# Row maxima of both query halves turned by one product with the identity, in a two-layer cross-attention

## The chip, the cores and the metric

The kernel runs on one core of a Trainium2 chip. The metric is the device time of one execution in microseconds (us). Three executions of the kernel before took 1470.49, 1475.73 and 1479.28 us; the median is 1475.73 us.

## The reference

Two cross-attention layers follow each other. There are 16 images; each has 256 queries of 320 channels (20 heads of 16 channels) and a context of 256 tokens of 512 channels. In the first layer the first 77 tokens are text and the remaining 179 are "image" tokens; in the second layer the last 4 tokens are the image tokens and 252 are text. Each layer computes, per head,

```
text  = softmax(q k_text^T / 4) v_text
image = softmax(q k_ip^T / 4 + 0.5 * sem) v_ip * mask
out   = (text + image) Wout + bout + residual
```

where `sem` is a further product between the text attention and the image tokens. For what is changed here only one thing matters: a softmax over the keys of a head, with the row maximum subtracted before the exponential. In the first layer the text part and the image part have a softmax each, so each query has two maxima per head; in the second layer one maximum over the 252 text keys is used.

## The kernel before, in words

The heads of an image are worked on in groups of four, so an image has five groups and a layer has 80 (`NS`). A group is called k: 0 to 79 belong to layer 0, 80 to 159 to layer 1. A layer's groups run one after the other in "slots". A slot also carries other work of the next and of the last images (projections, key and value products, the closing of an image); each such task has a list of due times in slots, and the function `fill` steps the tasks that are due.

The scores of a group are computed twice. First with the queries on the partitions: `score0` (layer 0, line 772 holds the products) and the second part of `both1` (layer 1, line 922) write four heads for one half of 128 queries (t = 0 or 1) to the two-bank tile `S`, and VectorE takes the maximum over the keys: lines 773 and 774 in layer 0 (text keys and image keys), line 923 in layer 1. The maxima go to a small tile `mn`. Second with the keys on the partitions: `turned0` (line 795) and the first part of `both1` (line 917) write to the banks `T`, and ScalarE takes the exponential (lines 798 and 929), which then goes to GpSimd (line 801 in layer 0, a product with `rs`) and as an operand into the value products (lines 833, 988 and 990).

For the second computation the maxima must lie along the free axis, as extra rows of the stacked queries `Q`, which meet a row of minus ones in the stacked keys `K`. That turn is made by `maxima0` (layer 0) and `maxima1` (layer 1): for each half t, a product that has `mn` as the stationary operand and the 128x128 identity as the moving one (lines 780 and 955) writes the half's 128 columns of an `X` bank; ScalarE copies the result to the tile `mt` (lines 782 and 957); and a DMA that ScalarE's queue issues (lines 783 and 959; the first group's is issued from SyncE's queue) writes it into two partitions of `Q`. `mt` has one buffer, `mn` has two.

The order of things around it. In slot k of layer 0 the list is: `maxima0(k+1)`, then `score0(k+2, 0)`, `turned0(k, 0)`, the value products of k-1, `score0(k+2, 1)`, `turned0(k, 1)`, and between them the tasks that are due. So the maxima that are turned in slot k are used at the start of slot k+1. In layer 1, `maxima1(k+2)` stands at the end of slot k, and its rows are used in slot k+2; its DMA may be held until the next slot's `release`. 

Who sets the order on each engine: TensorE's order is the order in which the program is written, in all stages. In the opening all queues go by the program. In layer 0's slots the orders of ScalarE, VectorE, GpSimd and SyncE are set when the kernel is built, by a planner that goes through the program with its own costs for each instruction; a few edges (`queued`, `anchor`) are fixed by hand. For example the second exponential of a slot is tied behind the DMA issue of line 783. In layer 1's slots TensorE, ScalarE, VectorE and GpSimd go by the program and SyncE by the planner. Most transfers are issued by SyncE through the helper at line 83. Line 260 is a helper for split products (three terms), line 632 the projections, line 709 a transpose of probabilities, line 975 the correction products of layer 1, and lines 187 and 188 a helper that splits a tile into a rounded part and a rest.

Of the kernel before, what the change touches and what calls it, by code (L numbers as in the profile page):

```python
# [9 lines left out]
FR = mybir.dt.float32r  # L10
AF = mybir.ActivationFunctionType
ALU = mybir.AluOpType
AX = mybir.AxisListType
# [4 lines left out]
S = 256  # L18
# [6 lines left out]
T0 = 77  # L25
NIP = 4
BI = B * NIP
T1 = S - NIP
# [21 lines left out]
def xattn2(  # L50
# [27 lines left out]
    nc = tc.nc  # L78
    f = lambda ap: ap.bitcast(F32)
    mm = nc.tensor.matmul  # L80
# [9 lines left out]
    def bank(tag="X"):  # L90
        return ps.tile([128, 512], F32, tag=tag, name=tag, bufs=BANKS[tag])

    def scores():

        return ps.tile([128, 1024], F32, tag="S", name="S", bufs=1).rearrange("p (h t) -> p h t", h=4)
# [5 lines left out]
    def buf(tag, shape, dtype=F32, bufs=1, name=None):  # L101
        if tag in ("wB", "wD", "vr", "raw"):
            return sb.tile(shape, dtype, tag=tag, name=name or tag, bufs=bufs)
        size = 1
        for d in shape[1:]:
            size *= d
        if tag not in slots:
            slots[tag] = [0, dtype] + [const_tile([128, max(size, words.get(tag, 0))], f"{tag}_{i}", dtype) for i in range(bufs)]
        n, kind, *ring = slots[tag]
        assert kind == dtype and len(ring) == bufs, tag  # L110
        slots[tag][0] += 1
        t = ring[n % bufs][: shape[0], :size]
        names = "abcd"[: len(shape) - 1]
        if len(names) > 1:
            t = t.rearrange(f"p ({' '.join(names)}) -> p {' '.join(names)}", **dict(zip(names, shape[1:])))
        return t
# [3 lines left out]
    def late(*makes):  # L120

        if held[0]:
            lates.extend(makes)
        else:
            for make in makes:
                make()
# [22 lines left out]
    def const_tile(shape, tag, dtype=F32):  # L149
        return const.tile(shape, dtype, tag=tag, name=tag)  # L150
# [8 lines left out]
    ident_r = const_tile([128, 128], "ident_r", FR)  # L159
# [15 lines left out]
    def anchor(inst):  # L175
        anchors[inst.ins.engine] = inst
        return inst
# [549 lines left out]
    casts = []  # L727
# [35 lines left out]
    maxes, issues = {}, {}  # L763

    def score0(k, t):
        Q, K = QK[k]
        if t == 0:
            maxes[k] = buf("mn", [128, 2, 2, 4], FR, bufs=2)
        mn = maxes[k]
        sp = scores()  # L770
        for h in range(4):
            mm(sp[:, h], Q[: XROW + T0, h, t * 128 : (t + 1) * 128], K[: XROW + T0, h], start=True, stop=True)  # L772
        nc.vector.tensor_reduce(mn[:, t, 0], sp[:, :, :T0], axis=AX.X, op=ALU.max)  # L773
        anchor(nc.vector.tensor_reduce(mn[:, t, 1], sp[:, :, T0:], axis=AX.X, op=ALU.max))  # L774

    def maxima0(k, queue=nc.scalar):
        Q, mn = QK[k][0], maxes[k]
        mp = bank()
        for t in range(2):
            mm(mp[:8, t * 128 : (t + 1) * 128], mn[:, t].rearrange("p a h -> p (a h)"), ident_r, start=True, stop=True)  # L780
        mt = buf("mt", [8, S], FR)
        casts.append(nc.scalar.copy(mt, mp[:8, :S]))
        issues[k] = queue.dma_start(f(Q[KS0 - 2 : KS0]), f(mt))

    def turned0(k, t):
# [117 lines left out]
    def both1(k, t):  # L903

        a = k + 2 < 2 * NS and QK[k + 2] 
        c = NS <= k < 2 * NS and QK[k]
        if a:
            if t == 0:
                maxes[k + 2] = buf("mn", [128, 4, 4], FR, bufs=2)[:, :2]
            sp = scores()  # L910
        if c:
            st = [bank("T").rearrange("p (h t) -> p h t", h=2) for u in range(2)]
            lo = (0, DUP)[t]
            for j in range(2):
                for u in range(2):
                    rows = slice(64 * u, 64 * u + KS1)
                    mm(st[u][:, j], c[1][rows, j, lo : lo + 128], c[0][rows, j], start=True, stop=True)  # L917
        if a:
            for j in range(2):
                for u in range(2):  # L920
                    rows = slice(64 * u, 64 * u + XROW)
                    mm(sp[:, 2 * u + j], a[0][rows, j, t * 128 : (t + 1) * 128], a[1][rows, j], start=True, stop=True)  # L922
            anchor(nc.vector.tensor_reduce(maxes[k + 2][:, t], sp[:, :, :T1], axis=AX.X, op=ALU.max))  # L923
            image_scores(k + 2 - NS, t, sp)
        if c:
            for u in range(2):
                if t == 0:
                    P[k, u] = buf("P", [128, 2, 2, S], bufs=SIZES["NP"]) if (k - NS) % 3 else last_stack([128, 2, 2, S], F32, u)
                anchor(nc.scalar.activation(P[k, u][:, t], st[u], AF.Exp, scale=SCALE))  # L929
# [3 lines left out]
    def image_scores(n, t, sp):  # L933
        b, g = divmod(n, NG)
        if (g, t) == (0, 0):
            sims[b] = buf("sr", [128, 2, 4, NG, NIP], bufs=2)
        sr = sims[b]
        src = sp.rearrange("p (u j) t -> p u j t", u=2)[:, :, :, T1:]
        anchor(queued(nc.vector.tensor_copy(sr[:, t, :, g].rearrange("p (j u) n -> p u j n", u=2), src)))
        if (g, t) == (NG - 1, 1):  # L940
            later(0.3, lambda: image_scores_out(b))
# [8 lines left out]

    def maxima1(k):
        mn = maxes[k]
        mp = bank()
        for t in range(2):
            mm(mp[:4, t * 128 : (t + 1) * 128], mn[:, t], ident_r, start=True, stop=True)
        mt = buf("mt", [8, S], FR)[:4]
        nc.scalar.copy(mt, mp[:4, :S])
        row = QK[k][0].rearrange("(u p) j t -> u p j t", u=2)[:, XROW]
        late(lambda: nc.scalar.dma_start(f(row), f(mt)))

# [32 lines left out]
    def slot1(k):  # L993
        last = k - 1 if NS < k <= 2 * NS else None
        mine = k < 2 * NS
        if k == NS:
            yield lambda: maxima(k + 1)
        yield lambda: both1(k, 0)
        if k == NS:
            yield lambda: attend0(k - 1)  # L1000
        summed = []
        if k > NS + 1:
            yield lambda: summed.append(attend1(k - 2))
        yield release
        yield lambda: both1(k, 1)
        if last:
            yield lambda: norm1(last, 0, 0)
# [223 lines left out]
    for c in range(B // 2):  # L1231
        n, k, b, d = 10 * c, [("k0", c)] if c else [], 2 * c, 2 * c + 1
# [39 lines left out]
    def ahead(k, t):  # L1272
        if k < NS:
            score0(k, t)
        else:
            both1(k - 2, t)

    def maxima(k):
        if k < 2 * NS:
            (maxima0 if k < NS else maxima1)(k)  # L1280
# [5 lines left out]
    def begin():  # L1286
# [36 lines left out]
        part("k0", 1)  # L1323
        stacks0(2, "T")
        score0(0, 0)
        part("k0", 0)
        part("v0", 1)
        score0(0, 1)
        part("v0", 1)
        maxima0(0, nc.sync)  # L1330
        part("k0", 1)
        part("v0", 1)
# [15 lines left out]
        stacks0(3, "M")  # L1348
        part("k0", 1)
        maxima0(1)  # L1350
        part("k0", 1)
        resid0.append(load(xT_d[0], "xc"))
# [117 lines left out]
```

## Time and profile before

| | |
|---|---|
| profiled execution, first to last instruction (span) | 1475.7 us |
| time of the executions | 1470.49, 1475.73, 1479.28 us |
| opening | about 0 to 60 us |
| slots of layer 0 | about 60 to 660 us, 7.5 us each |
| slots of layer 1 | about 660 to 1440 us, 9.75 us each |
| tail | about 1440 to 1476 us |
| busiest engines | TensorE 97%, VectorE 79%, GpSimd 78%, ScalarE 65% |
| mean granted TensorE clock | 0.993 |

The page gives no time for the profiled execution beside its span of 1475.7 us, which agrees with the middle one of the three times. Rows of groups read: line, engine and operation, output and inputs by the program's names, shapes, count, then durations in nanoseconds. PE is TensorE's matmul and PEld its weight load (the stationary operand), DVE is VectorE, ACT ScalarE, POOL GpSimd, SP SyncE; a q behind the name means the engine's instruction queue. Matmuls overlap each other in the records: a duration is longer than the distance from one start to the next, so a matmul's price is read from starts.

### The profile page before, as it was taken

Reading aid. Unit: us, or ns where it says so; the run is one execution under the profiler, and the core shown is the slowest. Engines: PE = TensorE matmul, PEld = TensorE weight load, DVE = VectorE, ACT = ScalarE, POOL = GpSimd, SP = SyncE. Lnnn points to the kernel's source line nnn. Section 1 sums busy time; section 2 is a strip of 40 time slices with the busy share of each in tenths; the row PEclk is TensorE's granted clock in tenths of the full one; section 3 lists DMA queues with packets and bytes.
Section 4 is the critical chain, followed back from the end, with each engine's and each line's share of the span. In section 5 each row is a group of like instructions: output and inputs, shape, how many; then the busy total and the mean of one; then the engine's idle time right before and its main releaser. Section 6 shows DMA issues by size and latency. Waiting matters only on the chain.

```text
span 1475.7 us, 35302 instructions
## 1 busy us (share of the span) xinstructions
PE 1433.6 (97%) x12438; PEld 1186.7 (80%) x12438; DVE 1166.0 (79%) x2569; ACT 956.5 (65%) x2074; POOL 1151.8 (78%) x1173
## 2 busy tenths in 40 slices
PE   6899999999999999799999999999999999999998
PEld 6788888888888878687778887888888888888865
DVE  5487676777677787967888888888888888888897
ACT  5577676767676776756666566656665666566553
POOL 4179797979797877987788877787778877887785
PEclk9999999999999999999999999999999999999999
DMA  6756565656656577565434433543354345433511
GB/s 196 194 160 184 134 184 141 184 143 165 162 154 164 144 195 205 140 184 158 138 102 140 146 119 101 161 146 102 118 161 146 89 131 161 135 101 116 150 32 50
DMA packets 230667, 211.78 MB, mean 144 GB/s; under 512 B 56314, under 2 KB 217116, under 8 KB 230492
## 3 DMA queue, kind: packets, MB, share of 16 engines
q1 hardware_dynamic: 229222, 208.56, 50.3%
q8 instruction: 99, 1.62, 0.5%
q10 hardware_dynamic: 1270, 0.98, 0.2%
q14 instruction: 76, 0.62, 0.1%
HBM read 122.07 MB, written 86.44 MB: 141 GB/s over the span
## 4 chain that ended last, share of the span: by engine, by line
PE 86%; DMA 4%; DVE 3%; POOL 3%; ACT 2%; issue 1%; SPq 0%; ACTq 0%; DVEq 0%; POOLq 0%
PE X L260 22%; PE X L975 18%; PE X L632 11%; PE P L833 7%; PE S L772 5%; PE P L988 5%; PE T L917 5%; PE T L795 4%; PE S L922 3%; PE P L990 2%; DMA kd<-kst 2%; PE X L1108 1%; POOL P L801 1%; PE X L690 1%; POOL wt L966 1%
## 5 line engine op out<-in xcount | busy, mean ns | idle before, releaser
L801 POOL TENSOR_TENSOR P<-P,rs 128x512 f32<-128x512 f32 x320 | 413.6, 1316 | 140.2 <-ACT P L798 140.2
L975 PE MATMUL X<-ctb,gm 128*128 128x512 f32 x1120 | 295.3, 407 | 0.0
L966 POOL TENSOR_TENSOR wt<-P,ctb 128x512 f32<-128x512 f32 x212 | 268.6, 1296 | 0.0
L923 DVE TENSOR_REDUCE mn<-S 128x4 fp32r<-128x1008 f32 x160 | 192.8, 1205 | 81.0 <-PE S L922 79.4
L975 PEld LDWEIGHTS X<-ctb,gm 128*128 128x128 f32 x1120 | 203.6, 190 | 49.4 <-issue 0.4
L798 ACT ACTIVATE P<-T 128x512 f32<-128x512 f32 x320 | 174.7, 593 | 100.5 <-PE T L795 81.0
L978 DVE TENSOR_TENSOR wt<-X,wt 128x512 f32<-128x512 f32 x240 | 159.3, 681 | 4.9 <-PE X L975 4.9
L929 ACT ACTIVATE P<-T 128x512 f32<-128x512 f32 x212 | 115.0, 597 | 54.5 <-PE T L917 41.6
L980 POOL TENSOR_TENSOR wt<-wt 128x512 f32<-128x512 f32 x80 | 103.6, 1295 | 58.3 <-DVE wt L978 58.3
L965 ACT ACTIVATE ctb<-P 128x512 fp32r<-128x512 f32 x212 | 122.5, 625 | 32.7 <-PE X L975 31.1
L774 DVE TENSOR_REDUCE mn<-S 128x4 fp32r<-128x716 f32 x160 | 142.4, 890 | 0.0
L833 PE MATMUL P<-P,vr 128*32 128x256 f32 x1920 | 123.8, 387 | 1.8 <-DVE tmp L850 0.8
L632 PE MATMUL X<-hq,wE 128*128 128x256 f32 x768 | 111.1, 289 | 4.4 <-ACT hq L615 3.9
L260 PE MATMUL X<-cta,wA 128*128 128x252 f32 (+3 forms) x726 | 104.2, 289 | 6.9 <-ACT wA L187 6.8
L632 PE MATMUL X<-ho,wF 128*128 128x256 f32 x768 | 106.6, 284 | 0.9 <-DVE ho L871 0.6
L632 PEld LDWEIGHTS X<-hq,wE 128*128 128x128 f32 x768 | 101.6, 195 | 7.2 <-ACT hq L615 4.4
L260 PEld LDWEIGHTS X<-cta,wA 128*128 128x128 f32 (+1 forms) x726 | 94.4, 191 | 10.7 <-ACT wA L187 7.0
L632 PEld LDWEIGHTS X<-ho,wF 128*128 128x128 f32 x768 | 98.7, 189 | 3.9 <-DVE ho L871 1.0
L844 DVE STREAM_TRANSPOSE nt<-P 128x512 f32<-128x512 f32 x80 | 57.0, 713 | 44.2 <-PE P L833 43.9
L773 DVE TENSOR_REDUCE mn<-S 128x4 fp32r<-128x308 f32 x160 | 74.5, 466 | 21.5 <-PE S L772 21.1
L833 PEld LDWEIGHTS P<-P,vr 128*32 128x32 f32 x1920 | 55.7, 110 | 42.7 <-issue 6.0
L772 PE MATMUL S<-ks,qs 125*128 125x256 f32 x480 | 87.0, 304 | 0.9 <-DVE mn L774 0.8
(223 smaller groups left out, 3279.7 us busy)
## 6 DMA issues: line engine op xcount, KB each, us to landing
qd<-q SPq DMA_DIRECT2D x48, 384.0 KB
kd<-kst SPq DMA_DIRECT2D x66, 256.0 KB
rawc<-in_cT_dram SPq DMA_DIRECT2D x60, 256.0 KB
qs<-qd SPq DMA_DIRECT2D x160, 96.0 KB
ks<-kd SPq DMA_DIRECT2D x160, 96.0 KB
qs<-qd SPq DMA_DIRECT2D x60, 192.0 KB
ks<-kd SPq DMA_DIRECT2D x60, 192.0 KB
qd<-q SPq DMA_DIRECT2D x32, 256.0 KB
```

Source lines behind the costliest of these rows:

```text
L260: last = mm(out, lhs(a, k), rhs(b, k), start=i == 0, stop=i == len(terms) - 1)
L632: mm(pp, w(s, k, slice(m * 128, (m + 1) * 128)), a[:, t], start=i == 0, stop=i == len(terms) - 1)
L772: mm(sp[:, h], Q[: XROW + T0, h, t * 128 : (t + 1) * 128], K[: XROW + T0, h], start=True, stop=True)
L774: anchor(nc.vector.tensor_reduce(mn[:, t, 1], sp[:, :, T0:], axis=AX.X, op=ALU.max))
L798: exp = anchor(nc.scalar.activation(pt, st[p], AF.Exp, scale=SCALE))
L801: anchor(nc.gpsimd.tensor_mul(pt, pt, rs[:, t : t + 1].to_broadcast([128, 2, S])))
L833: mm(pv[32 * s : 32 * s + 32, o : o + S], v[:, vt, h : h + 32], P[k, s // 2][:, t, s % 2], start=vt < 2, stop=vt != 1,)
L923: anchor(nc.vector.tensor_reduce(maxes[k + 2][:, t], sp[:, :, :T1], axis=AX.X, op=ALU.max))
L965: nc.scalar.activation(R[k, u][:, t], P[k, u][:, t], AF.Copy, scale=0.5)
L966: anchor(nc.gpsimd.tensor_sub(W[k, u][:, t], P[k, u][:, t], f(R[k, u][:, t])))
L975: mm(yp, gm[:, gb], R[k, u][:, kt], start=i == 0, stop=i == len(blocks[n]) - 1)
L978: nc.vector.tensor_mul(product, yp, w[:, n])
```

## The change

The maxima of both halves are kept side by side in `mn`, the half being the fastest index, and one product with the identity turns all of them: 16 stationary columns in layer 0 (two kinds of maxima, four heads, two halves) instead of twice 8, and 8 in layer 1 instead of twice 4. The product then has one partition for each head and half and 128 columns, where the two products before had one partition for each head and 256 columns. The copy to `mt` becomes 16x128 (before 8x256) and 8x128 (before 4x256). The DMA moves the same bytes into the same rows of `Q`, from 16 rows of 512 bytes instead of 8 of 1024 in layer 0, and from 8 rows of 512 bytes instead of 4 of 1024 in layer 1. VectorE's maxima write their four values with a step of two elements instead of one.

```diff
@@ def score0(k, t):
-            maxes[k] = buf("mn", [128, 2, 2, 4], FR, bufs=2)
+            maxes[k] = buf("mn", [128, 2, 4, 2], FR, bufs=2)
...
-        nc.vector.tensor_reduce(mn[:, t, 0], sp[:, :, :T0], axis=AX.X, op=ALU.max)
-        anchor(nc.vector.tensor_reduce(mn[:, t, 1], sp[:, :, T0:], axis=AX.X, op=ALU.max))
+        nc.vector.tensor_reduce(mn[:, 0, :, t], sp[:, :, :T0], axis=AX.X, op=ALU.max)
+        anchor(nc.vector.tensor_reduce(mn[:, 1, :, t], sp[:, :, T0:], axis=AX.X, op=ALU.max))
 
     def maxima0(k, queue=nc.scalar):
         Q, mn = QK[k][0], maxes[k]
-        mp = bank()
-        for t in range(2):
-            mm(mp[:8, t * 128 : (t + 1) * 128], mn[:, t].rearrange("p a h -> p (a h)"), ident_r, start=True, stop=True)
-        mt = buf("mt", [8, S], FR)
-        casts.append(nc.scalar.copy(mt, mp[:8, :S]))
+        mp = bank()[:16, :128]
+        mm(mp, mn.rearrange("p a h t -> p (a h t)"), ident_r, start=True, stop=True)
+        mt = buf("mt", [16, 128], FR)
+        casts.append(nc.scalar.copy(mt, mp))
         issues[k] = queue.dma_start(f(Q[KS0 - 2 : KS0]), f(mt))
@@ def both1(k, t):
-                maxes[k + 2] = buf("mn", [128, 4, 4], FR, bufs=2)[:, :2]
+                maxes[k + 2] = buf("mn", [128, 4, 2], FR, bufs=2)
...
-            anchor(nc.vector.tensor_reduce(maxes[k + 2][:, t], sp[:, :, :T1], axis=AX.X, op=ALU.max))
+            anchor(nc.vector.tensor_reduce(maxes[k + 2][:, :, t], sp[:, :, :T1], axis=AX.X, op=ALU.max))
@@ def maxima1(k):
         mn = maxes[k]
-        mp = bank()
-        for t in range(2):
-            mm(mp[:4, t * 128 : (t + 1) * 128], mn[:, t], ident_r, start=True, stop=True)
-        mt = buf("mt", [8, S], FR)[:4]
-        nc.scalar.copy(mt, mp[:4, :S])
+        mp = bank()[:8, :128]
+        mm(mp, mn.rearrange("p c t -> p (c t)"), ident_r, start=True, stop=True)
+        mt = buf("mt", [8, 128], FR)
+        nc.scalar.copy(mt, mp)
```

## The prediction

> **What bounds the kernel now.** I read the page first: its span, the busy shares and the chain of work that ended last.
>
> ```profile
> span 1475.7 us, 35302 instructions
> ...
> PE 1433.6 (97%) x12438; PEld 1186.7 (80%) x12438; DVE 1166.0 (79%) x2569; ACT 956.5 (65%) x2074; POOL 1151.8 (78%) x1173
> ...
> PE 86%; DMA 4%; DVE 3%; POOL 3%; ACT 2%; issue 1%; SPq 0%; ACTq 0%; DVEq 0%; POOLq 0%
> ```
>
> TensorE (PE) is busy 97% of the span and holds 86% of the chain. An average over stages can hide a stage with another limit, so I read the busy time by stretches next: two images of layer 0 at a time (columns: stretch, its length, then each engine's busy time with its count, granted clock, DMA share, GB/s).
>
> ```profile
> 140.00:215.00 75.00, 74.79 (x708) 64.55 (x707) 54.24 (x132) 54.30 (x118) 61.92 (x57) 1.00 0.61 159
> ...
> 441.00:517.00 76.00, 75.78 (x716) 65.51 (x715) 54.20 (x133) 55.76 (x121) 63.84 (x58) 1.00 0.61 157
> 517.00:592.00 75.00, 72.05 (x662) 61.68 (x661) 60.41 (x133) 51.51 (x113) 56.48 (x50) 0.98 0.73 203
> 592.00:660.00 68.00, 59.48 (x577) 48.65 (x576) 54.05 (x121) 45.63 (x96) 59.91 (x56) 0.97 0.62 163
> ```
>
> ```profile
> 760.00:1000.00 240.00, 240.00 (x2033) 193.62 (x2034) 206.50 (x429) 150.41 (x328) 193.50 (x212) 1.00 0.43 128
> 1000.00:1200.00 200.00, 200.00 (x1680) 162.09 (x1679) 171.60 (x361) 124.94 (x271) 158.51 (x173) 1.00 0.43 130
> ```
>
> From 140 to 517 us (five stretches, first and last shown) PE idles 0.2 us in 75; in layer 1 not at all. Only the end of layer 0 leaves it idle: 2.95 us in 517 to 592, 8.5 us in 592 to 660. So nearly everywhere a product taken from PE's list should shorten the time by the distance to the next product, as long as the other engines keep up; the next busiest engine has 14% to spare in layer 1 (DVE 206.50 of 240) and 16% in layer 0 (POOL 63.84 of 76).
>
> **The change part by part.** *1. One product less per group.* The tile of maxima, by form (durations least/median/greatest, then who waited for it: total us, times):
>
> ```profile
> L774 DVE TENSOR_REDUCE mn<-S x160: 877/891/899, 45.2 to 655.2; 128x4 fp32r<-128x716 f32 x160
> L780 PEld LDWEIGHTS X<-ident_r,mn x160: 85/88/138, 48.5 to 659.2; 128*8 128x8 f32 x160
> L780 PE MATMUL X<-ident_r,mn x160: 220/222/451, 48.6 to 659.2; 128*8 128x128 f32 x160
> L923 DVE TENSOR_REDUCE mn<-S x160: 1146/1207/1209, 660.2 to 1430.9; 128x4 fp32r<-128x1008 f32 x160
> L955 PEld LDWEIGHTS X<-ident_r,mn x160: 82/84/88, 666.3 to 1436.4; 128*4 128x4 f32 x160
> L955 PE MATMUL X<-ident_r,mn x160: 218/222/411, 666.4 to 1436.4; 128*4 128x128 f32 x160
> ...
>   PEld X L780: 7.4, 11
>   PE X L780: 3.7, 4
> ...
>   PEld X L955: 0.2, 1
> ```
>
> There are 160 products in each layer, two in each of 80 groups; 80 and 80 go. The 222 ns is a latency, since products overlap; the price is the distance between starts, which the order of time shows, one slot in each layer:
>
> ```profile
> 404.31 0.29 PE L780 MATMUL X<-ident_r,mn 128*8 128x128 f32 x2
> 404.43 0.68 PE L772 MATMUL S<-ksl,qsl 125*128 125x256 f32 x4
> 404.95 0.64 PE L795 MATMUL T<-qs,ks 127*128 127x256 f32 x4
> ```
>
> ```profile
> 1004.15 0.28 PE L955 MATMUL X<-ident_r,mn 128*4 128x128 f32 x2
> 1004.27 2.12 PE L632 MATMUL X<-ho,wF 128*128 128x256 f32 x16
> ```
>
> Two of them move the next product by 0.12 us in both layers, so one is 0.06 us. In layer 0, 15 groups (11 + 4) had PE wait for the maxima of line 774. There the first product ran in the shadow of the wait for the second half, and the single product will start when the second did: nothing is saved. Layer 1 has one such wait. So 65 x 0.06 = 3.9 us in layer 0 and 79 x 0.06 = 4.7 us in layer 1, together 8.6 us.
>
> The Trainium skill, "TensorE: Matmul & The Clock Gate", section "Wait — 56ns, not 53.3ns?", gives 55.6 ns from start to start for 128 moving columns on a warm array. The trace's 0.12 us for two agrees; by the page's figure the estimate would be 144 x 55.6 ns = 8.0 us, and I keep the rows' 8.6.
>
> *2. The weight load.* The remaining load has 16 or 8 columns instead of 8 or 4. The rows say 84 ns for 4 columns and 88 for 8, so about 1 ns per column and at most 8 ns more, beside the running product: 0. More delicate is the load that comes after it. The load for line 772 has 128 columns:
>
> ```profile
> 404.17 0.23 PEld L780 LDWEIGHTS X<-ident_r,mn 128*8 128x8 f32 x2
> 404.37 0.54 PEld L772 LDWEIGHTS S<-ksl,qsl 125*128 125x128 f32 x4
> ```
>
> ```profile
> 561.03 2.79 PE L260 MATMUL X<-kst,wB 128*128 128x64 f32 x24
> 563.75 2.58 PE L833 MATMUL P<-P,vr 128*32 128x256 f32 x24
> ```
>
> Where loads of 128 columns follow products of only 64 columns, 24 products take 2.72 us, 0.113 each: there the loads set the pace. Yet line 772's load starts at 404.37, with the second identity product, and its product starts at 404.43, 0.06 into a load that takes longer. So one identity product in front gives it all it had, and I count 0. The upper bound is 0.113 - 0.06 = 0.053 us in each of 160 groups, 8.5 us: the whole gain.
>
> The same page, section "Architectural detail: the array is 16× 32×32, not 1× 128×128", says that a matmul can begin before its weight load is complete. The two rows above agree (0.06 against 0.113), and it speaks for the 0.
>
> *3. ScalarE's copy and its DMA issue.*
>
> ```profile
> L782 ACT CAST mt<-X 8x256 fp32r<-8x256 f32 x80 | 28.4, 356 | 2.1 <-PE X L780 2.0
> ...
> L584 ACT CAST gm<-X 128x128 fp32r<-128x128 f32 x16 | 4.2, 265 | 2.7 <-PE X L260 2.7
> ```
>
> ```profile
> L959 ACTq DMA_DIRECT2D qs<-mt x80: 517/517/536, 667.9 to 1438.6; - x80
> L783 ACTq DMA_DIRECT2D qs<-mt x59: 620/621/1252, 64.9 to 651.3; - x59
> L783 ACTq DMA_DIRECT2D qsl<-mt x20: 621/621/650, 81.1 to 660.1; - x20
> ```
>
> The copy falls from 356 to about 265 ns (128 columns from the same banks), so ACT is busy 160 x 0.09 = 14 us less. The issue may grow: 4 rows take 517 ns and 8 take 621, which is 26 ns a row; 16 rows would then be 829 (+208, x79 = 16.4 us) and layer 1's 8 rows 621 (+104, x80 = 8.3 us), 24.7 us at most; if the issue goes by anything but rows, 0. In time:
>
> ```profile
> 405.10 0.78 ACT L744 CAST ks<-M 77x716 fp32r<-77x716 f32 x1
> 405.22 0.62 ACTq L783 DMA_DIRECT2D qs<-mt  x1
> ...
> 405.94 1.09 ACT L798 ACTIVATE P<-T 128x512 f32<-128x512 f32 x2
> ```
>
> The issue lies beside ACT's previous instruction (it ends at 405.84, that one at 405.88); with 0.21 us more, the exponential of line 798 would start some 0.2 us later where nothing waits for the issue otherwise. The exponential feeds GpSimd:
>
> ```profile
> L801 POOL TENSOR_TENSOR P<-P,rs 128x512 f32<-128x512 f32 x320 | 413.6, 1316 | 140.2 <-ACT P L798 140.2
> ```
>
> GpSimd waited 140.2 us for it, 1.75 us in each of 80 groups, so 0.2 us fits into its slack, and ACT carries 2% of the chain. I take 0 for copy and issue together, with the ends -1 and +24.7 us.
>
> *4. The DMA's way.* Twice the rows at half the size, the same 8 or 4 KB. The only landing on the chain is the first group's:
>
> ```profile
> 54.27 1.98 DMA qs<-mt
> ```
>
> In the slots what was issued at 405.22 is used by line 795 of the next slot:
>
> ```profile
> 411.42 0.28 PE L780 MATMUL X<-ident_r,mn 128*8 128x128 f32 x2
> ...
> 412.06 0.63 PE L795 MATMUL T<-qs,ks 127*128 127x256 f32 x4
> ```
>
> That is 6.8 us later; issue and landing take 0.62 + 1.98, so 4.2 us are spare, and twice the landing leaves 2.2. Layer 1 has a slot of 9.75 us. I take 0; at the first group the ends are 0 and +2 us.
>
> *5. VectorE.* Four values per partition are written with a step of two instead of one, out of 716 or 1008 read in 0.89 and 1.21 us; no row has such an output. Bounds: nothing, or the 14 ns between least and median of line 774 on 480 maxima, 6.7 us on an engine with 14% or more to spare: 0.
>
> *6. The planner.* In layer 0 the orders of ACT, DVE, POOL and SP are worked out again from other durations, in layer 1 SP's. Nothing in the trace shows the new order. A better one can win at most the idle time that PE has from 517 on, 2.95 + 8.5 = 11.5 us; a worse one can cost what the rivals below say. I take 0, with ends -11.5 and +46 (below).
>
> The sum is 1475.7 - 8.6 = 1467.1 us, against a profiled execution of 1475.7 that equals the median of the runs, 1475.73. So 1467, 0.6% faster. About 0.5% (7.4 us) is what a measurement of this kernel can tell from no change: faster is below 1468.4, slower above 1483.1.
>
> **The rivals.** *A new order that eats the gain (same).* If the five stretches from 140 to 517 (377 us) fall from 0.3% idle to the 3.9% of 517 to 592, that costs 13.6 us: 1467 + 13.6 = 1480.7; at half of it 1474. For it: four orders are planned anew, and a slip in one slot recurs in each of 80. Against it: PE's list is the same, and 16% of slack lies on each other engine. Centre 1475.
>
> *A new order that costs more (slower).* One mechanism: in layer 0 an engine's new order puts an instruction that waits ahead of one that PE needs, in each two images. It decides from (1483.1 - 1467) / 377 = 4.3% of PE idle; at the 12.5% of 592 to 660 it is 46 us, 1513; I take the middle, 8%, 30 us: 1497.
>
> *ScalarE's issue on the path (slower).* If all 24.7 us of part 3 delay PE: 1491.8; it decides from 16 of the 24.7. Against it stand ACT's 2% of the chain and GpSimd's 1.75 us.
>
> *The weight load uncovered (same).* The change then does not do what it says: 8.5 us are given back, 1475.6. The two rows of part 2 speak against it.
>
> **How the numbers follow.** My forecast, 1467, has 0.48, with its own range 1463 to 1471 (layer 1's 4.7 us alone give 1471; 4 us gained from idle PE time give 1463); 0.41 of it lies below 1468.4 and 0.07 above. The order that eats the gain has 0.21 (0.19 same, 0.02 faster), the order that costs more 0.20, the issue 0.05, the weight load 0.06 (same). Faster 0.43, same 0.32, slower 0.25. The range is 1461 to 1490: it takes in the first rival, the issue up to most of its price, and the cheaper third of the costly order; left out are about 0.13 above and 0.03 below.
>
> **What the profile after would show.** Lines 780 and its layer-1 like: 80 products each, and the next product 0.06 us after it; 160 fewer PE products. The slots of layer 1 should shrink by 0.06 us each with PE still without idle time: this is the surest part, 4.7 us between the same two groups. In layer 0, two-image stretches 0.5 to 0.6 us shorter if the new orders are harmless; if PE idles more than 0.3 us in them, the planner's rivals hold, and the waits name the engine. The copies near 265 ns; ACT's issues 829 and 621 if they go by rows. The prediction is wrong if PE's busy share between 140 and 517 falls under 99%, or if a product behind the identity product starts 0.11 us after it.

## The result, and the profile after

The changed kernel took 1477.94 us (median; 1474.06 to 1480.81), the kernel before 1475.94 us beside it (1470.49 to 1483.67). The ratio is 1.0008, with a 95% interval of 0.9998 to 1.0019: no difference that can be told, where 0.6% faster was forecast. The profiled execution of the changed kernel has a span of 1476.6 us, 0.9 more than that of before.

The page of the kernel after: span, busy shares, the shares of the chain of work that ended last, and the queue that carries the copies of the maxima (packets, megabytes, share).

```profile
span 1476.6 us, 35045 instructions
...
PE 1425.5 (97%) x12278; PEld 1176.7 (80%) x12278; DVE 1166.0 (79%) x2569; ACT 940.0 (64%) x2074; POOL 1150.2 (78%) x1173
...
q10 hardware_dynamic: 2222, 0.98, 0.3%
...
PE 86%; DMA 4%; DVE 4%; ACT 2%; POOL 2%; issue 2%; SPq 0%; ACTq 0%; DVEq 0%; POOLq 0%
```

The 160 products are gone (12438 to 12278) and TensorE is busy 8.1 us less, yet the span didn't shrink. So TensorE must idle more. The stretches of after (stretch, length, busy time of PE, PEld, DVE, ACT and POOL with counts, granted clock as a share of the full one, DMA share, GB/s), and with them the first part of layer 1, which the prediction had not looked at by itself:

```profile
140.00:215.00 75.00, 74.64 (x700) 64.46 (x700) 54.59 (x133) 53.44 (x120) 62.18 (x56) 1.00 0.62 160
441.00:517.00 76.00, 75.02 (x700) 64.50 (x698) 54.22 (x135) 55.36 (x120) 64.08 (x58) 1.00 0.60 156
517.00:592.00 75.00, 71.86 (x643) 60.97 (x644) 60.07 (x130) 48.57 (x111) 54.57 (x48) 0.95 0.72 198
592.00:660.00 68.00, 57.91 (x555) 47.16 (x555) 53.03 (x119) 43.86 (x93) 59.13 (x56) 0.95 0.63 160
660.00:776.00 116.00, 110.60 (x940) 86.59 (x939) 93.14 (x189) 71.38 (x158) 90.63 (x92) 1.00 0.44 130
760.00:1000.00 240.00, 238.33 (x2002) 191.47 (x2000) 206.17 (x430) 147.40 (x327) 193.89 (x212) 1.00 0.43 129
```

The same view of the kernel before, for the stretch that is new here:

```profile
660.00:776.00 116.00, 113.28 (x954) 89.49 (x954) 95.03 (x193) 73.76 (x159) 92.04 (x92) 0.99 0.44 130
```

TensorE idles 0.36 us from 140 to 215 and 0.98 from 441 to 517 (before 0.21 and 0.22), 10.1 us from 592 to 660 (before 8.5), 5.4 us from 660 to 776 (before 2.7), and 1.7 us from 760 to 1000, where before it never idled. The last two stretches lie in layer 1, where the prediction expected no idle time at all. Its reading "in layer 1 not at all" rested on 760 to 1200 us; in 660 to 776 TensorE idled 2.7 us already in before.

Because the stretches are not at the same place of the work in both kernels, I measured the same pieces of work instead: from the product with the identity in one group to that in a later group. For groups 92 and 156 (steady layer 1) these rows are, in the order of time of before, and then of after:

```profile
776.25 0.28 PE L955 MATMUL X<-ident_r,mn 128*4 128x128 f32 x2
...
1409.71 0.28 PE L955 MATMUL X<-ident_r,mn 128*4 128x128 f32 x2
```

```profile
778.26 0.22 PE L953 MATMUL X<-ident_r,mn 128*8 128x128 f32 x1
...
1410.19 0.22 PE L953 MATMUL X<-ident_r,mn 128*8 128x128 f32 x1
```

That is 633.46 us before and 631.93 after. The pieces from group 12 on in the same way (us; layer 1 begins with group 80; the names of the experiments are explained below). Each row is one profiled execution; the number in brackets is the granted clock where it was below 1.00 in the piece from group 80 to 92:

| kernel | groups 12 to 60 | 60 to 79 | 80 to 92 | 92 to 156 | 156 to the end |
|---|---|---|---|---|---|
| before | 360.7 | 150.2 | 109.8 (0.98) | 633.5 | 66.0 |
| after | 359.1 | 153.8 | 110.6 | 631.9 | 66.4 |
| wide_layer1 | 359.1 | 151.4 | 108.0 | 630.6 | 66.0 |
| before_pinned | 360.4 | 151.4 | 111.0 | 634.5 | 67.6 |
| after_pinned | 358.7 | 152.9 | 110.2 | 631.7 | 67.5 |
| after_pinned_again | 359.4 | 154.9 | 111.8 (0.98) | 631.7 | 67.5 |
| before_pinned_bank1 | 360.4 | 151.7 | 107.9 | 634.2 | 65.7 |
| after_pinned_bank1 | 358.8 | 150.5 | 107.7 | 631.3 | 65.6 |
| three_pinned | 362.8 | 151.2 | 111.3 | 637.6 | 66.7 |

Steady work did become shorter, by 1.6 us (48 groups) and 1.5 us (64 groups); the end of layer 0 became longer by 3.6, the start of layer 1 by 0.8 (although its clock was the better one), and the last part by 0.4. In layer 1 the waits of PE show what changed. The view of waits of after, from 665 us to the end (who waited for which tile of which engine: us, times, longest):

```profile
PE X L260 <- ACT mt L955: 2.0, 2, 1.1
...
PE X L1106 <- DVE wt L978: 1.2, 1, 1.2
...
PE X L632 <- DVE wt L978: 0.6, 1, 0.6
PE T L916 <- ACT mt L955: 0.5, 1, 0.5
```

The waits for `mt` and those of lines 1106 and 632 for `wt`, 4.3 us in five places, do not occur in before. The product of line 260 doesn't read `mt`; it writes into a PSUM bank (one of the pieces of the memory that takes TensorE's results), and `mt` is the copy that empties that bank. One of the two places, in the order of time of before and then of after:

```profile
766.89 1.15 ACT L965 ACTIVATE ctb<-ksl 128x512 fp32r<-128x512 f32 x2 [0.47 <-PE X L975]
...
767.10 0.28 PE L955 MATMUL X<-ident_r,mn 128*4 128x128 f32 x2
767.22 1.59 PE L260 MATMUL X<-cta,wA 128*128 128x252 f32 x12
...
767.95 0.30 ACT L607 ACTIVATE gm<-gm 128x128 fp32r<-128x128 f32 x1
768.15 0.34 ACT L957 CAST mt<-X 4x256 fp32r<-4x256 f32 x1
```

```profile
767.63 1.15 ACT L963 ACTIVATE ctb<-ksl 128x512 fp32r<-128x512 f32 x2 [0.45 <-PE X L973]
...
767.84 0.22 PE L953 MATMUL X<-ident_r,mn 128*8 128x128 f32 x1
...
768.68 0.29 ACT L607 ACTIVATE gm<-gm 128x128 fp32r<-128x128 f32 x1
...
768.88 0.24 ACT L955 CAST mt<-X 8x128 fp32r<-8x128 f32 x1
...
769.17 1.65 PE L260 MATMUL X<-cta,wA 128*128 128x252 f32 x12 [1.11 <-ACT mt L955]
```

In before the product of line 260 starts 0.12 us after the first identity product, long before the copy. In after it waits 1.11 us for the copy, which stands behind two instructions of line 963 and one of line 607 on ScalarE. The two kernels have the same order of instructions there; what differs is the bank that line 260 was given, as the experiments will show. One more wait of this kind lies at the end of layer 0 of after, and before has none there:

```profile
518.13 0.91 PE L260 MATMUL X<-cta,wA 128*128 128x192 f32 x6 [1.75 <-ACT mt L781]
```

The reason lies in how the kernel is built. The planner does not only set orders: it also hands out the PSUM banks, by its own idea of when each bank is read out. With the products and copies of the change it hands out other banks. By the lists of the two builds (the traces don't show a tile's bank) 268 of 1056 tiles `X`, 202 of 640 `T`, 43 of 160 `P` and 4 of 320 `S` stand in another bank than before; 402 of these tiles belong to layer 0 and 115 (60 `X`, 39 `T`, 16 `P`) to layer 1. The planned orders moved too (27 instructions on VectorE, 10 on ScalarE, 11 on SyncE and 2 on GpSimd, most of them between 510 and 660 us). So the result has three candidates: the orders of layer 0, the banks, and a product that is worth less than 0.06 us. A fourth thing, the granted clock, differs from one execution to the next; it is taken up at the end.

### The profile page after: what moved, and what is told of

It is laid out like the page before. It is cut to its first block, busy times and chain, and to the rows that moved or that the text cites. A ratio compares the mean times of both kernels' runs of the same rounds, so it can differ in the third digit from the quotient of the medians.

```text
span 1476.6 us, 35045 instructions
## 1 busy us (share of the span) xinstructions
PE 1425.5 (97%) x12278; PEld 1176.7 (80%) x12278; DVE 1166.0 (79%) x2569; ACT 940.0 (64%) x2074; POOL 1150.2 (78%) x1173
## 3 DMA queue, kind: packets, MB, share of 16 engines
q10 hardware_dynamic: 2222, 0.98, 0.3%
## 4 chain that ended last, share of the span: by engine, by line
PE 86%; DMA 4%; DVE 4%; ACT 2%; POOL 2%; issue 2%; SPq 0%; ACTq 0%; DVEq 0%; POOLq 0%
PE X L260 22%; PE X L973 17%; PE X L632 11%; PE P L832 7%; PE S L772 6%; PE P L986 5%; PE T L916 5%; PE T L794 5%; PE S L921 3%; PE P L988 2%; DMA kd<-kst 1%; PE X L690 1%; PE X L1106 1%; POOL P L800 1%; DMA qs<-qd 1%
## 5 line engine op out<-in xcount | busy, mean ns | idle before, releaser
L916 PEld LDWEIGHTS T<-qs,ks 49*128 49x128 f32 x640 | 50.3, 185 | 48.8 <-issue 22.2
```

## The experiments

All ratios are to the kernel before, run beside it on the same chip, with 95% intervals.

**Orders.** `after_order0` is after with the orders of before in layer 0 for ScalarE, VectorE, GpSimd and SyncE, written down as edges:

```diff
     with tc.manual_schedule(engines=PINNED):
         run(range(NS))
+        for e, text in ORDER.items():
...
+            turn = [made[e][i] for i in turn if begins[e] <= i < len(made[e])]
+            for one, two in zip(turn, turn[1:]):
+                tc.add_manual_dep(
+                    two.ins, one.ins.name, mybir.DependencyInfo(mybir.DependencyClass.NoSync, mybir.DependencyReason.DATA), reason="order"
+                )
```

`ORDER` holds each engine's order of before as text. The banks of layer 0 are planned anew with these orders.

> The changed kernel, but in layer 0's slots ScalarE, VectorE, GpSimd and SyncE keep the order that the planner had given them for the kernel before; the PSUM banks are left to the planner. Theory A (the planner's new plan, orders and banks, ate the gain of the removed products): the 3.4 us that were lost between 517 and 660 us come back, about 1474 us in all, 0.1 to 0.3% under the kernel before. Theory B (the removed products are worth nothing at the end, since some other engine or transfer sets the pace of the transitions whatever the plan): as the changed kernel, 1477 to 1478 us.

Measured: 0.9984 (0.9973 to 0.9994), 1474.93 us. Layer 1 still has the waits of after, the two of the split product (line 260 of after) for `mt` among them, 2.0 us. Between the ratios of after and of this kernel lie 0.24% (3.5 us), each ratio being uncertain by some 0.1%: less than the 0.6% that was missing. Whether the orders explain even this is taken up below.

**The copy's length.** `after_wide_copy` leaves one product per group and doubles ScalarE's copy by reading the 128 columns twice; the DMA sends the first half.

```diff
-        mt = buf("mt", [16, 128], FR)
-        casts.append(nc.scalar.copy(mt, mp))
-        issues[k] = queue.dma_start(f(Q[KS0 - 2 : KS0]), f(mt))
+        mt = buf("mt", [16, 2, 128], FR)
+        casts.append(nc.scalar.copy(mt, mp.unsqueeze(1).to_broadcast([16, 2, 128])))
+        issues[k] = queue.dma_start(f(Q[KS0 - 2 : KS0]), f(mt[:, 0]))
...
-        mt = buf("mt", [8, 128], FR)
-        nc.scalar.copy(mt, mp)
+        mt = buf("mt", [8, 2, 128], FR)
+        nc.scalar.copy(mt, mp.unsqueeze(1).to_broadcast([8, 2, 128]))
...
-        late(lambda: nc.scalar.dma_start(f(row), f(mt)))
+        late(lambda: nc.scalar.dma_start(f(row), f(mt[:, 0])))
```

> The changed kernel, but the copy to mt writes its 128 columns twice (16x256 and 8x256, as long as before); the DMA reads the first 128. With that copy the planner gives layer 1's tiles the banks that the kernel before had. Theory A: the two waits of TensorE for the copy at 720 and 767 us are gone (about 2 us), some 1475 to 1476 us, and TensorE's lag against the kernel before falls through layer 1 without a rise at 767. Theory B: the longer copy brings back nothing, 1477 to 1479 us. Theory C (the half-size rows of the DMA cost the time): as the changed kernel, 1477 to 1478 us, since the rows stay at 512 bytes.

Measured: 0.9973 (0.9957 to 0.9989), 1472.21 us: more work on ScalarE, and faster than after by more than was expected (1475 to 1476). The half-size rows of the DMA are still in it, so they aren't what costs. In its build all tiles of layer 1 have the banks of before. To tell the copy from the plan and one layer from the other, each layer was done alone. `wide_layer1` has the doubled copy in layer 1 only; its plan of layer 0 is exactly that of after, and the banks of layer 1 are those of before. `wide_layer0` has it in layer 0 only; the banks of layer 1 stay those of after. `wide_order0` is `after_wide_copy` with the orders of before in layer 0.

> The changed kernel with the double-width copy to mt in layer 1 alone (8x256). Layer 0's orders and banks are then exactly those of the changed kernel, and layer 1's banks those of the kernel before. Theory A1 (layer 1's banks cost part of the gain): the waits of TensorE for the copy at 720 and 767 us go, 2 to 3 us under the changed kernel, so 0.05 to 0.15% under the kernel before. Theory A0 (only layer 0's plan costs): within 1 us of the changed kernel, 0.0 to 0.15% over the kernel before.

> The changed kernel with the double-width copy to mt in layer 0 alone (16x256). Layer 0's orders and banks are then those of after_wide_copy, layer 1's banks those of the changed kernel. Theory A1: the two waits for the copy at 720 and 767 us stay, so 2 to 3 us slower than after_wide_copy, about 0.1% under the kernel before. Theory A0: as fast as after_wide_copy, 0.27% under the kernel before.

> after_wide_copy (layer 1's banks as in the kernel before) with the order of layer 0's slots written down as the planner had given it for the kernel before; only layer 0's banks are planned anew. If orders and layer 1's banks are all that ate the gain: what the change is worth with its plan held, 0.35 to 0.55% under the kernel before, 1469 to 1472 us. If layer 0's banks matter as much as its orders: no faster than after_wide_copy, 0.2 to 0.3% under the kernel before.

Measured: `wide_layer1` 0.9961 (0.9946 to 0.9976), 1470.5 us; `wide_layer0` 0.9997 (0.9986 to 1.0007), 1475.62 us; `wide_order0` 0.9961 (0.9947 to 0.9975), 1470.24 us. The gain is in layer 1, and it is larger than the 0.05 to 0.15% under before that the two waits for `mt` had suggested: 0.39%. It needs no order of layer 0: `wide_layer1` has the orders of after. The tile `mt` and the place shown above, in `wide_layer1`:

```profile
L955 ACT CAST mt<-X x80: 339/356/361, 664.4 to 1430.8; 8x256 fp32r<-8x256 f32 x80
```

```profile
762.62 0.22 PE L953 MATMUL X<-ident_r,mn 128*8 128x128 f32 x1
...
762.68 1.59 PE L260 MATMUL X<-cta,wA 128*128 128x252 f32 x12
...
763.67 0.35 ACT L955 CAST mt<-X 8x256 fp32r<-8x256 f32 x1
```

The copy takes 356 ns instead of 249, is as late on ScalarE as in after, and nobody waits for it: line 260 starts 0.06 us after the identity product. The five waits are gone from this kernel's view of waits. The longer copy lengthens ScalarE's work; what it changed to the better is the plan, since by its build the planner now gives each tile of layer 1 the bank of before. So the length of this copy, as the planner counts it, decides about the banks. The interval of `wide_layer1` lies wholly under 1 and under the interval of after, so it is the fastest kernel of the three, though by less than the 0.5% that the prediction asked of a difference.

**The change with the plan held.** To price the product alone, `before_pinned` and `after_pinned` have the same orders and the same bank for each tile (the orders of before in layer 0, the banks of after). All banks are one tile, and a list says which part each tile gets:

```diff
+    whole = ps.tile([128, 4096], F32, tag="W", name="W", bufs=1)
+
     def bank(tag="X"):
-        return ps.tile([128, 512], F32, tag=tag, name=tag, bufs=BANKS[tag])
+        b = int(next(places[tag]))
+        return whole[:, 512 * b : 512 * b + 512]
```

> The kernel before with two things written down by hand: in layer 0's slots the order that the planner had given ScalarE, VectorE, GpSimd and SyncE for it, and for every PSUM tile of the program the bank that the planner gave it in the changed kernel. Theory A: slower than the kernel before by what those banks cost alone, 1 to 6 us (1477 to 1482 us), with TensorE waiting for the copies to mt. Theory B: 1475 to 1477 us.

> The changed kernel with the same orders and the same banks written down as in before_pinned, so that only the change itself differs between the two. Theory A: 7 to 9 us (0.5 to 0.6%) faster than before_pinned. Theory B: within 2 us of before_pinned.

Measured: `before_pinned` 1.0045 (1.0030 to 1.0061), 1482.53 us; `after_pinned` 1.0010 (0.9998 to 1.0023), 1478.78 us. The change is worth 0.35% (5.2 us) here, between the two outcomes that had been expected (7 to 9 us, or under 2). And before, with its own products and its own orders of layer 0, is 0.45% slower with the banks of after, written down, than as it was built. `three_pinned` turns the sign: `before_pinned` with a third product of the identity per group into unused columns of the same bank, whose result nothing reads (layer 1's is shown; layer 0 has the like).

```diff
...
         for t in range(2):
             mm(mp[:4, t * 128 : (t + 1) * 128], mn[:, t], ident_r, start=True, stop=True)
+        mm(mp[:4, 2 * 128 : 3 * 128], mn[:, 1], ident_r, start=True, stop=True)
```

> before_pinned with a third product with the identity in each group (into unused columns of the same bank), orders and banks as there. It measures what one product is worth at the end of the run with the plan held. If 0.06 us on TensorE's path each: 8.6 to 9.6 us over before_pinned, 1.010 to 1.011 times the kernel before. If the end feels only the part that after_pinned gained (5.2 us): 1.008. If products are hidden: 1.0045.

Measured: 1.0079 (1.0064 to 1.0095), 1488.69 us, by the ratios 0.34% (5.0 us) above `before_pinned`. A slot of layer 1 in the order of time of `three_pinned`:

```profile
1009.80 0.28 PE L996 MATMUL W<-ident_r,mn 128*4 128x128 f32 x2
1009.92 0.22 PE L997 MATMUL W<-ident_r,mn 128*4 128x128 f32 x1
1009.98 2.12 PE L672 MATMUL W<-ho,wF 128*128 128x256 f32 x16
```

The third product also costs 0.06 us where it stands, 160 x 0.06 = 9.6 us in all; 5.0 arrive. In these banks one product less and one more agree: some 5 us.

**The banks alone.** `before_pinned_bank1` and `after_pinned_bank1` have the 115 tiles of layer 1 in the banks of before; the rest of the lists stays, as do the orders, but for one move on SyncE. The edit is 115 digits of the list of parts. `after_pinned_again` repeats `after_pinned` beside them.

> before_pinned with the same 115 tiles in the banks that layer 1 has in the kernel before. If the banks cost the kernel before as much as the changed one: 4 to 7 us under before_pinned, about 1.000 times the kernel before, and 5 us over after_pinned_bank1. If banks and change act on each other: no faster than before_pinned, 1.004.

> after_pinned (the changed kernel with the narrow copy, orders and banks written down) with 115 of its PSUM tiles, all in layer 1, moved to the banks that layer 1 has in the kernel before; the length of the copy and the orders stay. If it is the banks and not the longer copy that made wide_layer1 fast: 4 to 7 us under after_pinned, 0.996 to 0.998 times the kernel before, and no wait of TensorE for the copy to mt at 720 and 767 us. If the longer copy did it in another way: as after_pinned, 1.000 to 1.002.

> after_pinned once more, on the chip of the other two, as the measure for the first: 1.000 to 1.002 times the kernel before by all theories.

Measured: `before_pinned_bank1` 1.0010 (0.9999 to 1.0020), 1477.67 us; `after_pinned_bank1` 0.9961 (0.9947 to 0.9975), 1471.71 us; `after_pinned_again` 1.0009 (1.0000 to 1.0019), 1477.75 us. So the two causes stand beside each other:

| ratio to before | layer 1 in the banks of after | layer 1 in the banks of before | what the banks cost |
|---|---|---|---|
| two products (before) | 1.0045 | 1.0010 | 0.35%, 5.2 us |
| one product (after) | 1.0010 and 1.0009 | 0.9961 | 0.48%, 7.1 us |
| what the change brings | 0.35%, 5.2 us | 0.49%, 7.2 us | |

A single ratio is uncertain by 0.10 to 0.16%, so the two figures of a kind don't differ with certainty, but each is well above zero. The 1.0010 of before with its own banks in layer 1 leaves at most 0.2% for the 402 tiles of layer 0 and for the writing down itself, taken together.

The waits show the mechanism. The view of waits of PE from 665 us to the end, of `after_pinned` (all banks are `W` there):

```profile
PE W L300 <- ACT mt L69: 2.0, 2, 1.1
...
PE W L1146 <- DVE wt L69: 0.7, 1, 0.7
PE W L672 <- DVE wt L69: 0.6, 1, 0.6
PE W L956 <- ACT mt L69: 0.5, 1, 0.5
```

None of these four is in `after_pinned_bank1`. The same place in the tail, the last group's identity product and what follows it, in `after_pinned` and then in `after_pinned_bank1`:

```profile
1431.09 0.41 PE L993 MATMUL W<-ident_r,mn 128*8 128x128 f32 x1
1432.16 0.70 PE L1146 MATMUL W<-rs,rs 128*128 128x256 f32 x2 [0.66 <-DVE wt L69]
1433.38 0.50 PE L956 MATMUL W<-qs,ks 49*128 49x256 f32 x4 [0.52 <-ACT mt L69]
```

```profile
1428.48 0.41 PE L993 MATMUL W<-ident_r,mn 128*8 128x128 f32 x1
1428.72 0.65 PE L1146 MATMUL W<-rs,rs 128*128 128x256 f32 x2
1429.30 0.50 PE L956 MATMUL W<-qs,ks 49*128 49x256 f32 x4
```

From the identity product to the scores of line 956 it is 2.29 us with the banks of after and 0.82 with those of before. The first part of layer 1 shows the banks in busy time too, again in `after_pinned` and then in `after_pinned_bank1`:

```profile
660.00:776.00 116.00, 110.22 (x929) 86.78 (x932) 94.65 (x193) 71.82 (x159) 92.72 (x94) 1.00 0.43 128
660.00:776.00 116.00, 112.96 (x962) 89.15 (x961) 97.40 (x196) 73.40 (x162) 95.37 (x95) 1.00 0.45 137
```

TensorE idles 5.8 us and 3.0. All thirteen profiles divide by this: 5.1 to 5.9 us of idle time in the seven whose layer 1 has the banks of after, 2.7 to 3.2 in the six with those of before, whatever their orders, products and copies. In the table of pieces, where the clock was 1.00, the banks cost 3.1 us (the pinned pair with two products) or 2.6 (with one) between groups 80 and 92, 0.3 to 0.4 between 92 and 156, and 1.9 from group 156 to the end. That is 5.3 us with two products, against 5.2 by the ratios, and 4.9 with one, against 7.1; what the ratios have beyond this is not in these profiles.

## Why the prediction was wrong

**Where it failed: part 6, the planner, which the sum took at 0.** The prediction priced the planner by what new orders could do, those of layer 0 above all. The planner also hands out banks, and that in both layers, and of this the sum has no term. The other banks of layer 1 took 5.2 us back (measured with two products) to 7.1 (with one), in the slots that the prediction had called its surest part, with PE still without idle time. The ends of the term were wide enough (-11.5 and +46), but the place and the mechanism were missing. The shorter copy stood in part 3, as a gain of 14 us on ScalarE that costs nothing; that the planner also goes by its length was not followed up.

**A second step was mis-sized: the sum of part 1.** The change is worth 5.2 to 7.2 us with the plan held, where the sum has 8.6.

**Part 1, the price of a product: right at its place, too large in sum.** In after the next product follows at the forecast distance:

```profile
402.56 0.22 PE L779 MATMUL X<-ident_r,mn 128*16 128x128 f32 x1
402.62 0.69 PE L772 MATMUL S<-ksl,qsl 125*128 125x256 f32 x4
```

But 0.06 us saved in a slot do not all reach the end of the slot. In `after_pinned` against `before_pinned` the 48 groups from 12 on bring 1.0 to 1.8 us instead of 2.9, the 64 groups from 92 on 2.8 instead of 3.8, and the 19 groups from 60 on nothing that can be told (152.9 and 154.9 against 151.4 us). The prediction had inferred from a PE without idle time that each product taken out counts in full. In layer 0 a part comes back as waiting. The waits of PE in after, 140 to 517 us:

```profile
PE X L779 <- DVE mn L774: 1.2, 5, 0.3
```

The view of before is empty there: five weight loads of line 780 waited for the maxima (1.7 us), but PE had the other half's product to run meanwhile. Now PE waits 0.24 us in each of five groups, so one wait takes back the saving of several groups. The prediction had seen such groups, but counted only their own product as lost. (It also counted 15 of them where 11 stand: the four waits of a product are in the same groups as four of the weight loads, so its own sum should be 8.9.) With the orders held it is the same: the idle time of groups 12 to 60 is 0.6 us in `before_pinned`, and 1.3 and 2.1 in the two profiles of `after_pinned`; that of groups 60 to 79 is 12.6, and 14.0 and 15.9. Where the rest of the steady price goes, some 1 us in the 64 groups of layer 1 above all, stays open.

**Part 2, the weight load: right.** 0.06 us again, not 0.113; the rival of the uncovered load falls.

**Part 3, ScalarE: right for its engine.** The copy takes 250 ns, where 265 was estimated. The issue, whose price by rows was the upper end, does not go by rows: 16 rows in layer 0 take what 8 took, 8 rows in layer 1 what 4 took. The tile `mt` of after, with those who waited for it:

```profile
L781 ACT CAST mt<-X x80: 236/250/257, 49.5 to 661.0; 16x128 fp32r<-16x128 f32 x80
L955 ACT CAST mt<-X x80: 232/249/254, 668.3 to 1437.7; 8x128 fp32r<-8x128 f32 x80
L957 ACTq DMA_DIRECT2D qs<-mt x80: 517/518/543, 668.9 to 1437.9; - x80
L782 ACTq DMA_DIRECT2D qs<-mt x59: 620/621/1259, 64.9 to 653.0; - x59
...
  PE T L794: 4.8, 1
...
  PE X L260: 3.8, 3
```

The upper end of 24.7 us, and the rival built on it, fall with this. The last row has the new waits of line 260 for the bank, two in layer 1 and one in layer 0: the cost is tied to the copy that became shorter.

**Parts 4 and 5: right.** The packets of the queue rose from 1270 to 2222, as the rows doubled, and nothing came of it: the first group's wait is 4.8 us after 4.6. The maxima written with a step of two take no longer: the medians are 893 and 1208 ns, after 891 and 1207.

**The rivals.** "A new order that eats the gain" named the time (1474 to 1480.7) and the planner, but the wrong thing that it plans and the wrong layer: between 140 and 517 us PE idles 2.4 us in 377, where that rival needed 3.9%, and `wide_layer1` is 0.4% faster than before with those orders in place. The prediction's own sign for the planner's rivals, more than 0.3 us of idle time in two images, did show (0.36, and 0.98 from 441 to 517), but it misled: the wait behind it, for VectorE's maxima, stands in `after_pinned` too (1.0 us in four places), which has the orders of before.

**What stays open.** The end of layer 0. Groups 60 to 79 took 153.8 us in after and 150.2 in before, which alone is more than the missing time of the profiled execution. But after and `wide_layer1`, with one plan there and the bank wait of 1.75 us in both, took 153.8 and 151.4. They idle alike (13.9 and 14.0 us, before 11.5); what differs is the clock: from 517 to 660 us TensorE ran at half clock for 13.7 us in after, and for 6.8 in `wide_layer1` as in before. So of the 3.6 us some 2.4 go with the clock of that one execution, and some 1.2 are left where the clock is alike. The bank wait itself is absent where layer 0 has the doubled copy (`wide_layer0`, `after_wide_copy`) and where it has the orders of before. What the orders cost can't be told from this. `after_order0` against after suggests 0.24%, but its executions also had the higher clock (0.994 in the mean, against 0.991 for after and 0.993 for before), and whether the orders bring that about was not tried. `wide_order0` against `after_wide_copy` gives 0.12% with intervals that overlap, and `wide_layer1` is as fast as `wide_order0` without them.

## What to carry to other kernels

Where a planner hands out buffers, an edit that only shortens an instruction can, as here, decide which later instruction shares its buffer. So look in the order of time at the product behind the edited one, and at what stands ahead of the reader of its bank on the reader's engine: rows in which an instruction waits for a tile that it does not read are such a wait. Before a gain of a few microseconds is believed or given up, hold orders and buffers fixed in both kernels, and price the edit in the other direction too (one product more). And put the granted clock and the idle time beside each piece of a single profile before its length is compared.

## What the runs showed that was not expected

- A bank matters more than the edit: 115 tiles of layer 1 in other banks cost 5.2 to 7.1 us of some 1476, as much as 160 products.
- The issue time of these transfers on ScalarE's queue was 621 ns for 8 and for 16 rows in layer 0, and 517 ns for 4 and for 8 rows in layer 1.
- The same program varies by microseconds in one piece, and idle time and clock have to be told apart in it. The two executions of `after_pinned` took 95.3 and 97.8 us for the first 12 groups, at a granted clock of 1.00 and 0.98; at the end of layer 0 they took 152.9 and 154.9 us at 0.97 both, and there the idle time differs (14.0 and 15.9 us). In all kernels the slower executions tend to have the lower mean clock. The falls come in stretches at half clock, and one begins at the end of the longest wait of PE after the opening, of line 709 near 600 us, which took 2.94 us in before and 3.90 in after. The stretch of before and then that of after:

```profile
601.60:605.00 3.40, 3.40 (x20) 2.63 (x24) 1.71 (x3) 2.47 (x7) 2.50 (x4) 0.50 0.18 54
601.30:608.10 6.80, 6.08 (x38) 3.94 (x39) 2.91 (x7) 4.74 (x12) 5.23 (x6) 0.50 0.12 33
```

  The Trainium skill, "TensorE: Matmul & The Clock Gate", Part 1, says that the clock is either full or half and is set by how busy the array was in windows of some 3.4 us that run on their own. The traces agree: the stretch of before lasts 3.4 us, that of after 6.8. So where a wait falls among the windows may decide how long the stretch is (`wide_layer1` waited 4.4 us there and had 3.4 at half clock), which is a possible cause of this variation; no run tried it.
